# Two layers of message passing on a graph: 56 of the 98 tiles of the table relu(LN(x))·W0 made inside the loop of the first block, not ahead of it

## The chip, the cores and the metric

One Trainium2 chip, one core. The number is the device time of one execution in microseconds (us), as a median over runs. The engines are TensorE (PE, with its weight loads as PEld), VectorE (DVE), ScalarE (ACT), GpSimd (POOL) and SyncE (SP). Each works through its own list of instructions in order and waits for others by semaphores. POOL issues the gathers and scatters (indirect DMAs), SP issues the plain DMAs.

## The reference

There are N = 12500 nodes of D = 256 numbers and E = 200000 edges (`src`, `dst`, sorted by `dst`). The distribution of `dst` is dense at small numbers: it is 12500·u² of a uniform u.

```python
h = relu(layernorm(x))
x = x + segment_sum(edge_weight[:, None] * (h @ W0)[dst], src, N)      # layer 0
h = relu(layernorm(x))
q, k, v = h @ Wq.T + bq, h @ Wk.T + bk, h @ Wv.T + bv                  # 8 heads of 32
sim = (q[dst] * k[src]).sum(-1) / sqrt(32)                             # layer 1
attn = softmax of sim over the edges with the same dst
x = x + segment_sum(attn * v[src], dst, N) @ Wo.T + bo
```

## The kernel before

The edges are cut into 391 groups of 512, and the groups into four blocks of 128 (the last block has 7). The order of the instructions on PE, DVE, ACT, POOL and SP is written out by hand, that is, it is the order of the Python calls in `layer0` and `layer1`. What one call issues stands on each engine behind what the calls ahead of it issued there.

**The stretch ahead of the gathers** (`layer0`, the loop `while rest or live`). Three things run interleaved. `sort(0)` sorts block 0 by `src`: some 130 stages, each of them three compares on DVE (L237, L240, L241), a copy of the values on ACT (`vp`, L235) and a predicated copy on DVE (L247). At the larger distances the tile is transposed: 8 transposes on PE, and copies out of PSUM on ACT (L280, L282) or DVE (L265). `hidden()` makes the table HW = relu(x − mean)·W0 / sd, 98 tiles of 128 nodes, in 25 chunks of four tiles, at 85 steps of 100. Per tile it takes the sum and the squares on ACT (L569, L580; for one tile in four `bn_stats` on DVE, L572), subtracts the mean on POOL (`norm`, L596), transposes on PE (`turn`, L602), copies with relu on ACT (`turned`, L607), multiplies on PE (`mult`, L613) and copies with the factor 1/sd on ACT (`put`, L619). Per chunk there is one load and one store on SP. `group_l0` does the 7 groups of the last block, which are not sorted, with scatters on POOL. The first gather needs `dT` (L291), which the sort leaves.

**The loop of layer 0** (`for t in range(NGS + 6)`) has 120 + 128 + 128 steps. In block 0 a step has three tiles of 128 sorted edges, in blocks 1 and 2 four. Step t issues the gathers of step t + 4 on POOL (`load_s`, L648; six buffers `hg`), makes the one-hot matrices of step t + 1 on DVE (`onehot_s`, L657, which read `iop`, a row of numbers in a PSUM bank), multiplies gathered rows and one-hots on PE (`sum_s`, L668, and L667 for the last row of the window ahead), copies the window to `wn` for that (ACT, L689) and adds it to rows of an accumulator (`store_s`, DVE L694), which SP loads (`window_s`) and stores. Beside this runs the sort of the next block, 1.2 stages a step in block 0 and 1.14 in block 1, from step 4 of the block on. From t = 66 to 236 there are also 152 "hot" tiles, edges with `dst` below 128, whose rows come from a matrix product with the first 128 rows of HW (`hot_load`, `hot_ones`, `hot_pair`, `hot_apply`, `hot_add`, `hot_store`); those 128 rows are loaded over `w0[:, 0]` ahead of the loop. `prep_s` prepares layer 1 at t = 154, 174, 194 and 214. In block 2 `project_s` makes K and V of each finished window and stores them (`put`, L737, through two buffers `K`).

**Layer 1** has 391 steps and 1564 gathers of K and V (L978, 15 buffers `kvt`). Its last part merges the rows at the ends of the groups (`merge_steps`). There `same`, at step NG − 2, makes matrices that say which group ends are the same node (L1199 to L1210) and a mask (L1213 to L1216). These live in buffers of the tile `kvt`.

Of the kernel before, what the change touches and what calls it, by code (L numbers as in the profile page):

```python
# [18 lines left out]
P = 128  # L19
G = 512  # L20
# [37 lines left out]
H0, H1 = 66, 236  # L58
# [23 lines left out]
class Gnn:  # L82
# [30 lines left out]
    def sort_consts(self, it, ic):  # L113
        nc, kp = self.nc, self.k0
        ev = kp.tile([P, 1], I32, name="ev")
        nc.vector.tensor_scalar(ev, ic, 1, None, op0=ALU.bitwise_and)
        self.sgn = kp.tile([P, 1], F32, name="sgn")
        nc.vector.tensor_scalar(self.sgn, ev, -2.0, 1.0, op0=ALU.mult, op1=ALU.add)
        gr = kp.tile([P, P], I32, name="gr")
        nc.vector.tensor_scalar(gr, it, 1, None, op0=ALU.logical_shift_right)  # L120
        nc.vector.tensor_tensor(gr, gr, it, op=ALU.bitwise_xor)
        self.turn = kp.tile([P, 7, P], F32, name="turn")
        for j in range(7):
            bt = kp.tile([P, P], I32, name="bt", bufs=2)
            nc.vector.tensor_scalar(bt, gr, j, 1, op0=ALU.logical_shift_right, op1=ALU.bitwise_and)
            nc.vector.tensor_scalar(self.turn[:, j], bt, -2.0, 1.0, op0=ALU.mult, op1=ALU.add)
        self.iop = self.tp.tile([P, G], F32, name="iop")[:, :P]
        nc.vector.tensor_copy(self.iop, self.iof)
# [44 lines left out]
    def prep_c(self, b):  # L173
# [22 lines left out]
        ci = self.csi[b] = cp.tile([P, P, W], I32, name=f"ci{b}")  # L196
# [13 lines left out]
    def sort(self, b):  # L210
# [86 lines left out]
        if b == 0:  # L297
            nc.scalar.copy(self.in_order(eT), self.by_col(V))
            yield
# [61 lines left out]
    def tile_bases(self, dT, sf, eT, turned):  # L361
# [11 lines left out]
        self.fm = k0.tile([P, 9], F32, name="fm0")  # L373
        nc.vector.memset(bs[:, NHT:NHT + 1], float(BIAS))
# [16 lines left out]
    def hot_prep(self):  # L391
        nc, k0, wp = self.nc, self.k0, self.wp
        dT, eT, sT, _, _ = self.part[0]
        bs, fm, n = self.hb, self.fm, NHT
        nc.vector.memset(bs[:, 0:1], float(HBIAS))
# [18 lines left out]
        nc.vector.tensor_reduce(self.fl[:, 0, 0:1], fm[:, :8], op=ALU.max, axis=AX.X)  # L414
# [28 lines left out]
    def hot_apply(self, j):  # L443
        self.nc.tensor.matmul(self.hp[j][:, D:], self.ha.pop(j)[:, 0], self.w0[:, 0], start=True, stop=True)
# [89 lines left out]
    def hidden(self):  # L534
# [4 lines left out]
        chunks = list(range(nch - 2, nch)) + list(range(nch - 2))  # L539
        seq = [i for c in chunks for i in range(c * HC, min(nt, (c + 1) * HC))]  # L540

# [51 lines left out]
        def norm(i):  # L593
            c, j, r = tile_of(i)
            h = T[i]["h"] = wp.tile([P, D], F32, name="h", bufs=3)
            nc.gpsimd.tensor_scalar(h[:r], X[c][:r, j], M[c][:r, j, 0:1], None, op0=ALU.add)  # L596

        def turn(i):
            r = tile_of(i)[2]
            pt = T[i]["pt"] = tp.tile([P, G], F32, name="pt", bufs=1)[:, :D].rearrange("p (k e) -> p k e", e=P)  # L600
# [8 lines left out]
        def mult(i):  # L609
            r = tile_of(i)[2]  # L610
            ph = T[i]["ph"] = self.bank()[:, :D]
# [3 lines left out]
        def put(i):  # L615
# [4 lines left out]
            if j == HC - 1 or i == nt - 1:  # L620
                v, n = rows(self.HW, c)
                nc.sync.dma_start(v, Y[c][:, :n])
                if r < P:
# [8 lines left out]
        for s in range(nt + 8):  # L632
            for f, k in fs:
                if 0 <= s - k < nt:
                    f(seq[s - k])
            yield

# [5 lines left out]
    def load_s(self, g):  # L643
# [3 lines left out]
        for w, (c, _) in enumerate(self.tiles(b, p)):  # L647
            nc.gpsimd.indirect_dma_start(out=hg[:, w], out_offset=None, in_=self.HW,  # L648
                                         in_offset=bass.IndirectOffsetOnAxis(ap=self.part[b][0][:, c:c + 1], axis=0))
# [41 lines left out]
    def store_s(self, g):  # L691
# [5 lines left out]
        if b == NPT - 1:  # L697
            self.X[g] = dict(x=ws, base=v)
# [5 lines left out]
    def project_s(self, t):  # L704
# [30 lines left out]
        def put(X):  # L735
            kv = wp.tile([P, G], F32, name="K")
# [170 lines left out]
    def prep_s(self, b):  # L907
# [27 lines left out]
        self.nsl[b] = self.kp.tile([P, P, W], F32, name=f"nsl{b}")  # L935
# [7 lines left out]
        nc.sync.dma_start(self.PD[b * 2 * P:(b + 1) * 2 * P].rearrange("(p c) -> p c", c=2), gb[:, 1:3])  # L943
        nc.vector.tensor_tensor(t, pf, df, op=ALU.is_gt)
# [216 lines left out]
    def merge_steps(self):  # L1161
# [19 lines left out]
        def loads():  # L1181
            b = big(2 * KB * P)
            pdr, S = b[:, :KB * P], b[:, KB * P:].rearrange("p (k e) -> p k e", k=KB)
# [7 lines left out]

        def same():
            pdr, S, pdc = T["pdr"], T["S"], T["pdc"]
            cnt = wp.tile([P, KB], F32, name="cntm", bufs=1)
            tr = wp.tile([P, KB], F32, name="trm", bufs=1)
            scr = wp.tile([P, P], F32, name="scrm", bufs=1)
            T["idx"] = wp.tile([P, KB], I32, name="idxm", bufs=1)
            T["nid"] = wp.tile([P, KB], I32, name="nidm", bufs=1)
            nc.vector.tensor_scalar(T["nid"], pdc, 0.0, None, op0=ALU.max)  # L1199
            T["C"] = big(KB * P, KB)  # L1200
            for k in range(KB):
                r, m = size(k), pdr[:, rows(k)]
                if k:
                    nc.vector.tensor_scalar(T["C"][:, k], m, pdc[:, k - 1:k], self.ident[:, size(k - 1) - 1:size(k - 1)],
                                            op0=ALU.is_equal, op1=ALU.mult)
                nc.vector.tensor_scalar(S[:, k, :r], m, pdc[:, k:k + 1], None, op0=ALU.is_equal)
                nc.vector.scalar_tensor_tensor(scr[:, :r], S[:, k, :r], 1.0, self.lower[:, :r], op0=ALU.mult, op1=ALU.mult,
                                               accum_out=cnt[:, k:k + 1])
            nc.vector.tensor_scalar(tr, cnt, 0.0, self.trash, op0=ALU.is_gt, op1=ALU.mult)
            nc.vector.tensor_tensor(T["idx"], tr, pdc, op=ALU.max)  # L1210
            b = big(2 * NR + 2)
            mk, f = b[:H, :NR + 1], b[:H, NR + 2:]
            nc.vector.memset(mk[:, 0:1], NEG)  # L1213
            nc.vector.memset(mk[:, NR:], NEG)
            nc.vector.tensor_tensor(mk[:, 1:NR], pdr[:H, 1:NR], pdr[:H, :NR - 1], op=ALU.not_equal)
            nc.vector.tensor_scalar(mk[:, 1:NR], mk[:, 1:NR], NEG, None, op0=ALU.mult)  # L1216
# [39 lines left out]
        def total(k):  # L1256
# [8 lines left out]
            if k:  # L1265
                q = size(k - 1)
                nc.tensor.matmul(pg[:r], T["C"][:q, k, :r], T["ms"][:q, k - 1], start=False, stop=True)
# [18 lines left out]
        def ends_put(k):  # L1286
# [6 lines left out]
        steps = [((NG - 3, 0), loads), ((NG - 2, 0), same), ((NG - 1, 0), load_rows), ((NG, 1), own_rows),  # L1293
                 ((NG + 1, 0), lambda: space("ms", D + H)), ((NG + 2, 0), lambda: space("o", D)),
                 ((NG + 4, 0), factors), ((NG + 4, 2), factor_cols), ((NG + 4, 2), lambda: space("an", D)),
                 ((NG + 5, 0), lambda: space("at", D)), ((t + 1, 0), load_rest)]
        for k in range(KB):
# [177 lines left out]
    def layer0(self):  # L1475
        tc, nc = self.tc, self.nc
        ET = mybir.EngineType
        with tc.tile_pool(name="k0", bufs=1) as self.k0, tc.tile_pool(name="w0", bufs=2) as self.wp, \
# [28 lines left out]
            with tc.manual_schedule(engines={ET.SP, ET.PE, ET.DVE, ET.Activation, ET.Pool}):  # L1507
# [6 lines left out]
                rest = [self.KS, self.hidden()]  # L1514
                s, gs, live = 0, [], None
                while rest or live:
                    for f in list(rest):
                        if (f is self.KS or s * 85 % 100 < 85) and next(f, self) is self:
                            rest.remove(f)
# [20 lines left out]
                nc.sync.dma_start(self.w0[:, 0], self.HW[:P])  # L1540
# [3 lines left out]
                job, quota, hq, hl = None, 0.0, [], 0  # L1544
                for t in range(NGS + 6):
                    b, p = sblk(t) if t < NGS else (NPT, t - NGS)
                    due = min(NHT, max(0, round((t - H0) * NHT / (H1 - H0))))
                    if hq:
# [12 lines left out]
                    if job is not None and p > 3:  # L1561
                        quota += 1.2 if b == 0 else 1.14
                        while quota >= 1.0:
                            quota -= 1.0
                            if next(job, self) is self:
                                job, quota = None, 0.0
                                break
                    if t + 2 < NGS and (sblk(t + 2)[0] < 2 or b == 2 and p > 0):
# [23 lines left out]
                    if todo_hot:  # L1592
                        self.hot_apply(hj)
                        if hj + 1 < NHT:
                            self.hot_ones(hj + 1)
                    self.project_s(t)
                    for f in todo.get(t, []):
                        f()
                    if t >= 122 and t % 2 == 0 and fill2:
                        fill2.pop(0)()  # L1600
                assert self.hs == NHT and not hq
                assert job is None and not fill and not fill2

    def run(self, hook=lambda k, n: None):
# [3 lines left out]
        with ExitStack() as es:  # L1608
# [7 lines left out]
            self.HW = self.dp.tile([N, D], F32, name="HW")  # L1616
            self.SL = self.dp.tile([NG, G], U8, name="SL")
# [5 lines left out]
            self.AG = self.dp.tile([N + P, D + H], F32, name="AG")  # L1623
            self.fl = cp.tile([P, NBLK, 2], F32, name="fl")
# [52 lines left out]
```

## Time and profile before

| | us |
|---|---|
| median of 12 runs (4285.13 to 4302.65) | 4292.26 |
| the profiled execution | 4303.72 |
| its span, first to last instruction | 4301.7 |
| first gather of layer 0 (start) | 357.2 |
| last gather of layer 0 (start) | 2122.9 |
| first and last gather of layer 1 (start) | 2150.4 and 4190.0 |

| engine | busy us | share |
|---|---|---|
| PE | 3459.6 | 80% |
| DVE | 3406.4 | 79% |
| POOL | 2985.0 | 69% |
| ACT | 2205.4 | 51% |

The profile is of one execution. Busy time is the union of an engine's instructions; a wait is the idle time ahead of an instruction, put down to what ended last. A 32-bit matmul shows as two passes, so the 1384 products of gathered tiles show as 2768.

### The profile page before, as it was taken

The numbers are of one execution on the slowest core, as the hardware profiler recorded it, in microseconds if no ns is written. First come the engines' busy times: TensorE is split into PE (matmuls) and PEld (weight loads), VectorE is DVE, ScalarE is ACT, GpSimd is POOL, SyncE is SP. The second block draws the span as 40 slices with busy tenths as digits, with TensorE's granted clock in tenths as the row PEclk, the third lists the DMA queues.
The fourth block names the chain that finished last, engine by engine and source line by source line (L and its number), as shares of the span: only waits on it lengthen the run. The fifth ranks groups of instructions, "written<-read, shape, count | busy, mean of one in ns | idle before, by whom it ended". The sixth has DMA issues, their size and how long they took to land. (4 is left out here: it accounts for less than half of the span.)

```text
span 4301.7 us, 61889 instructions
## 1 busy us (share of the span) xinstructions
PE 3459.6 (80%) x14078; PEld 2309.5 (54%) x14078; DVE 3406.4 (79%) x7226; ACT 2205.4 (51%) x6200; POOL 2985.0 (69%) x3096
## 2 busy tenths in 40 slices
PE   3665678786777789999868888888888888888886
PEld 2443335454444444444456666666666666666664
DVE  7878989697898666666558878788888888888895
ACT  5664345343443222222236666666666666666663
POOL 2555777677776777777567777777777777777771
PEclk9888999898998899999969999999999999999998
DMA  6434667786776788888688989889988888888892
GB/s 203 105 99 140 179 187 228 210 241 193 218 222 199 217 237 250 251 239 236 207 242 270 281 269 277 276 276 282 281 270 282 275 280 271 273 263 266 278 291 77
DMA packets 627547, 1004.38 MB, mean 233 GB/s; under 512 B 97274, under 2 KB 450359, under 8 KB 627165
## 3 DMA queue, kind: packets, MB, share of 16 engines
q0 software_dynamic: 196224, 596.49, 47.9%
q1 hardware_dynamic: 430941, 403.79, 29.3%
q8 instruction: 119, 1.95, 0.2%
q14 instruction: 263, 2.15, 0.2%
HBM read 788.60 MB, written 224.47 MB: 236 GB/s over the span
## 5 line engine op out<-in xcount | busy, mean ns | idle before, releaser
L978 POOL DMA_INDIRECT kvt<-KV,ci x1564 | 1501.5, 960 | 565.7 <-issue 405.9
L648 POOL DMA_INDIRECT hg<-HW,dT x1384 | 1314.9, 950 | 469.2 <-issue 355.2
L668 PE MATMUL pg<-hg,ohs 128*128 128x256 f32 x2768 | 875.7, 424 | 191.7 <-DMA hg<-HW,dT 80.4
L1089 PE MATMUL pg<-pv,oh 128*82 128x264 f32 x3126 | 845.3, 418 | 19.8 <-DVE pv L1077 16.6
L668 PEld LDWEIGHTS pg<-hg,ohs 128*128 128x128 f32 x2768 | 474.8, 197 | 585.3 <-DMA hg<-HW,dT 220.4
L1011 PE MATMUL pq<-qt,oht 80*128 80x256 f32 x3128 | 771.5, 391 | 8.1 <-ACT oht L987 8.1
L1011 PEld LDWEIGHTS pq<-qt,oht 80*128 80x128 f32 x3128 | 615.4, 198 | 117.7 <-ACT oht L987 9.3
L1089 PEld LDWEIGHTS pg<-pv,oh 128*82 128x82 f32 x3126 | 507.1, 165 | 257.0 <-issue 65.3
L1012 DVE TENSOR_TENSOR pr<-pq,kvt 128x512 f32<-128x512 f32 x782 | 514.4, 684 | 160.7 <-PE pq L1011 153.4
L995 ACT ACTIVATE oh<-iof,nsl 128x82 f32<-128x82 f32 x1564 | 437.3, 350 | 261.4 <-PE pg L1089 259.6
L657 DVE TENSOR_SCALAR ohs<-iop,sT,eT 128x128 f32<-128x128 f32 x1384 | 475.3, 410 | 39.8 <-PE pg L668 39.8
L1077 DVE TENSOR_TENSOR pv<-kvt,pp 128x1024 f32<-128x1024 f32 x391 | 471.4, 1206 | 34.4 <-ACT pb L1066 34.4
L1013 DVE TENSOR_REDUCE sim<-pr 128x32 f32<-128x1024 f32 x391 | 477.1, 1220 | 13.4
L986 ACT ACTIVATE oht<-slt,npcol 80x512 f32<-80x512 uint8 x391 | 281.9, 721 | 103.6 <-PE pq L1011 56.1
L689 ACT COPY wn<-pg 128x256 f32<-128x256 f32 x373 | 138.4, 371 | 279.7 <-PE pg L668 279.6
L471 ACT ACTIVATE sd<-mv,eps 128x1 f32<-128x1 f32 x128 | 37.7, 295 | 470.3 <-DVE sd L476 459.6
L827 PE MATMUL pq<-wtq,qh 128*128 128x256 f32 x392 | 133.7, 473 | 159.1 <-DMA qh<-HT 131.6
L987 ACT ACTIVATE oht<-oht 80x512 f32<-80x512 f32 x391 | 246.3, 630 | 12.7
L247 DVE COPY_PREDICATED W<-m,vp 128x512 f32<-128x512 int32 x317 | 232.6, 734 | 18.7 <-ACT vp L235 18.5
L715 PE MATMUL tps<-wkv,ht 128*128 128x512 f32 x512 | 240.7, 593 | 0.0
L737 DVE TENSOR_TENSOR K<-tps,bias 128x512 f32<-128x512 f32 x128 | 88.6, 692 | 185.0 <-PE tps L715 182.2
L235 ACT COPY vp<-W 128x512 f32<-128x512 f32 x344 | 203.2, 591 | 61.7 <-DVE W L247 50.9
(304 smaller groups left out, 4558.3 us busy)
## 6 DMA issues: line engine op xcount, KB each, us to landing
KV<-K SPq DMA_DIRECT2D x128, 256.0 KB
AG<-ag SPq DMA_DIRECT2D x391, 82.5 KB
tw<-acc SPq DMA_DIRECT2D x248, 128.0 KB
acc<-ws SPq DMA_DIRECT2D x248, 128.0 KB
qt<-Q SPq DMA_DIRECT2D x391, 80.0 KB
kvt<-KV,ci POOLq DMA_INDIRECT x1564
hg<-HW,dT POOLq DMA_INDIRECT x1384
xh<-acc SPq DMA_DIRECT2D x152, 128.0 KB
```

The lines of the kernel that those rows point to most:

```text
L648: nc.gpsimd.indirect_dma_start(out=hg[:, w], out_offset=None, in_=self.HW, in_offset=bass.IndirectOffsetOnAxis(ap=self.part[b][0][:, c:c + ...
L657: self.nc.vector.tensor_scalar(oh[:, w], self.iop, sT[:, c], eT[:, c], op0=ALU.is_equal, op1=ALU.mult)
L668: nc.tensor.matmul(pg, oh[:, w], hg[:, w], start=(w == 0), stop=(w == n - 1))
L978: nc.gpsimd.indirect_dma_start(out=kv[:, w], out_offset=None, in_=self.KV, in_offset=bass.IndirectOffsetOnAxis(ap=self.csi[b][:, p, w:w + ...
L986: nc.scalar.activation(oht, sl, AF.Abs, bias=self.npcol[:QW])
L987: nc.scalar.activation(oht, oht, AF.Relu, bias=1.0, scale=-1.0)
L995: nc.scalar.activation(oh[:, w], self.iof[:, :MA], AF.Abs, bias=self.nsl[b][:, p, w:w + 1])
L1011: nc.tensor.matmul(pq[:, c], oht[:, 2 * a + c], qt, start=True, stop=True)
L1012: nc.vector.tensor_mul(pr[:, 2 * a:2 * a + 2], pq, kv[:, 2 * a:2 * a + 2, :D])
L1013: nc.vector.tensor_reduce(sim[:, :, i, :], pr.rearrange("p w (h d) -> p w h d", h=H), op=ALU.add, axis=AX.X)
L1077: self.nc.vector.tensor_tensor(pv[:, :, :D].rearrange("p w (h d) -> p w h d", h=H), kv[:, :, D:].rearrange("p w (h d) -> p w h d", h=H), s ...
L1089: nc.tensor.matmul(pg, oh[:r, w], pv[:r, w], start=(w == 0), stop=(w == nw - 1))
```

## The change

The table is made in two parts. Ahead of the loop `hidden` now makes 42 tiles only: the last two chunks (6 tiles), which `group_l0` needs, and the first nine (36 tiles). It runs in every step of the sort up to 24 and then in 40 of 100. The first three chunks (1536 rows) are also stored to a table of their own, HA. Block 0 gathers from HA, by `dA`, which is `dT` cut off at 1535; a flag (`far`) sends inputs with larger `dst` there to the general path. The other 56 tiles are made in the loop of layer 0, from t = 5 to 80, by `table(pos, t)` at three places of a step: `mult` at the start, the statistics, `norm` and `put` after the sort's stages, `turn` and `turned` at the end. In these tiles `norm` is on ACT, and the transposed tile and the product lie in the free columns of the PSUM bank of `iop`, one after the other. The hot tiles start at t = 84 rather than 66; their 128 rows have a tile of their own. K and V are stored through four buffers (`K` and `W`) rather than two. In layer 1 `same` is cut into seven parts, at steps 296 + 9k, which write over parts of `nsl` and `ci` that are no longer read; the mask is made in `prep_s` and loaded.

```diff
-H0, H1 = 66, 236
+H0, H1 = 84, 236
+NHA = 12
+HT0, HT1 = 5, 81
+NHS = 6
...
-        self.iop = self.tp.tile([P, G], F32, name="iop")[:, :P]
+        self.iopt = self.tp.tile([P, G], F32, name="iop")
+        self.iop = self.iopt[:, :P]
...
             nc.scalar.copy(self.in_order(eT), self.by_col(V))
+            self.dA = self.l0r.bitcast(I32)
+            nc.vector.tensor_scalar(self.dA, dT, float(NHA * P - 1), None, op0=ALU.min)
...
+        far = wp.tile([P, G], F32, name="pf", bufs=1)
+        nc.vector.tensor_tensor(far, dT, self.dA, op=ALU.not_equal)
+        nc.vector.tensor_reduce(fm[:, 8:9], far, op=ALU.max, axis=AX.X)
...
-        chunks = list(range(nch - 2, nch)) + list(range(nch - 2))
+        na = NHA // HC
+        first = list(range(nch - 2, nch)) + list(range(na + NHS))
+        chunks = first + list(range(na + NHS, nch - 2))
         seq = [i for c in chunks for i in range(c * HC, min(nt, (c + 1) * HC))]
+        ns = sum(min(nt, (c + 1) * HC) - c * HC for c in first)
+        late = set(seq[ns:])
...
-            nc.gpsimd.tensor_scalar(h[:r], X[c][:r, j], M[c][:r, j, 0:1], None, op0=ALU.add)
+            if i in late:
+                nc.scalar.activation(h[:r], X[c][:r, j], AF.Identity, bias=M[c][:r, j, 0:1])
+            else:
+                nc.gpsimd.tensor_scalar(h[:r], X[c][:r, j], M[c][:r, j, 0:1], None, op0=ALU.add)
...
-            pt = T[i]["pt"] = tp.tile([P, G], F32, name="pt", bufs=1)[:, :D].rearrange("p (k e) -> p k e", e=P)
+            T[i]["pp"] = self.iopt[:, P:P + D] if i in late else tp.tile([P, G], F32, name="pt", bufs=1)[:, :D]
+            pt = T[i]["pt"] = T[i]["pp"].rearrange("p (k e) -> p k e", e=P)
...
-            ph = T[i]["ph"] = self.bank()[:, :D]
+            ph = T[i]["ph"] = T[i]["pp"] if i in late else self.bank()[:, :D]
...
                 nc.sync.dma_start(v, Y[c][:, :n])
+                if c < na:
+                    nc.sync.dma_start(rows(self.HA, c)[0], Y[c][:, :n])
...
+        ls = ((mult, 7, 0), (root, 3, 1), (scale, 4, 1), (stats, 0, 1), (square, 2, 1), (norm, 5, 1), (put, 7, 1),
+              (turn, 6, 2), (turned, 6, 2))
+        n = nt - ns
+        for s in range(n + 7):
+            for pos in range(3):
+                for f, k, at in ls:
+                    if at == pos and 0 <= s - k < n:
+                        f(seq[ns + s - k])
+                yield
...
-            kv = wp.tile([P, G], F32, name="K")
+            kv = wp.tile([P, G], F32, name="KW"[X["g"] % 2])
...
+        me = wp.tile([P, 2], F32, name="me")
+        nc.vector.tensor_tensor(me[:, 0:1], pf[:, 0:1], base, op=ALU.not_equal)
+        nc.vector.tensor_copy(me[:, 1:2], ne)
+        nc.vector.tensor_scalar(me, me, NEG, None, op0=ALU.mult)
+        nc.sync.dma_start(self.ME[b * 2 * P:(b + 1) * 2 * P].rearrange("(p c) -> p c", c=2), me)
...
+        def same(k):
+            S, pdc, cnt = T["S"], T["pdc"], T["cnt"]
+            r, m = size(k), T["pdr"][:, rows(k)]
+            scr = wp.tile([P, P], F32, name="scrm", bufs=1)
+            nc.vector.tensor_scalar(S[:, k, :r], m, pdc[:, k:k + 1], None, op0=ALU.is_equal)
+            nc.vector.scalar_tensor_tensor(scr[:, :r], S[:, k, :r], 1.0, self.lower[:, :r], op0=ALU.mult, op1=ALU.mult,
+                                           accum_out=cnt[:, k:k + 1])
+            if k:
+                q = size(k - 1)
+                nc.vector.tensor_scalar(m, m, pdc[:, k - 1:k], self.ident[:, q - 1:q], op0=ALU.is_equal, op1=ALU.mult)
...
-        steps = [((NG - 3, 0), loads), ((NG - 2, 0), same), ((NG - 1, 0), load_rows), ((NG, 1), own_rows),
+        steps = [((286, 1), loads), ((366, 0), own_ids), ((NG - 2, 0), load_mask), ((NG - 1, 0), load_rows), ((NG, 1), own_rows),
...
+        steps += [((296 + 9 * k, 0), lambda k=k: same(k)) for k in range(KB)]
...
-                    for f in list(rest):
-                        if (f is self.KS or s * 85 % 100 < 85) and next(f, self) is self:
-                            rest.remove(f)
+                    if going:
+                        going = next(self.KS, self) is not self
+                    if not self.ready and (s < 24 or s * 40 % 100 < 40 or not going):
+                        next(HT)
...
+                def table(pos, t):
+                    nonlocal late, made
+                    goal = (3 * (NQ - NHA - 2 - HC - HC * NHS) + 21) * (t - HT0 + 1) / (HT1 - HT0)
+                    while late and made < goal and (pos is None or made % 3 == pos):
+                        made += 1
+                        late = next(HT, self) is not self
+                        if pos is not None:
+                            break
```

## The prediction

> **What bounds the kernel now.** I read the waits of POOL first, then POOL's timeline, then the windows by stage, then DVE's waits ahead of the first gather, and last DVE's timeline at the end.
>
> The timeline of POOL in block 0 (start, duration, engine, line, operation, idle before):
>
> ```profile
> 562.68 0.95 POOL L648 DMA_INDIRECT hg<-HW,dT  x1 [0.30 <-issue]
> 563.93 0.95 POOL L648 DMA_INDIRECT hg<-HW,dT  x1 [0.30 <-issue]
> 565.18 0.95 POOL L648 DMA_INDIRECT hg<-HW,dT  x1 [0.30 <-issue]
> ```
>
> Gathers start every 1.25 us. POOL shows 76% busy (0.95 of 1.25) when it cannot go faster, so its 69% hides the bound. The waits of POOL over the whole span (in total, times, longest):
>
> ```profile
> POOL kvt L978 <- issue: 405.9, 1332, 0.3
> POOL hg L648 <- issue: 355.2, 1166, 0.3
> POOL kvt L978 <- DVE pv L1077: 84.0, 75, 7.9
> POOL hg L648 <- PE pg L668: 50.2, 65, 7.0
> ...
> POOL hg L648 <- DVE dT L291: 17.5, 1, 17.5
> ```
>
> The 0.3 us waits for "issue" are part of the rhythm. 1384 gathers at 1.2545 us are 1736 us, and from the first (357.2) to the last (2122.9) it is 1766: POOL lost some 30 us in all of layer 0. Layer 1 is alike: 1564 at 1.2545 are 1962 of 2040 us. So three things set the time: when the first gather starts, how often a late consumer blocks POOL, and the end after the last gather at 4190. The windows by stage (length; busy us and instructions of PE, PEld, DVE, ACT, POOL; clock; DMA share and GB/s):
>
> ```profile
> 8.90:357.20 348.30, 196.26 (x820) 145.43 (x820) 277.06 (x774) 229.59 (x679) 153.83 (x126) 0.85 0.46 125
> 357.20:836.30 479.10, 356.93 (x1383) 204.61 (x1383) 422.31 (x1193) 199.96 (x528) 357.56 (x378) 0.92 0.67 197
> 836.30:1495.60 659.30, 485.92 (x2048) 304.75 (x2047) 534.22 (x1502) 248.85 (x701) 481.72 (x506) 0.88 0.74 214
> ```
>
> Ahead of the gathers DVE is the bound (277 of 348 us). In block 0 POOL's 357.6 us at 76% are 470 of 479 us; DVE is at 88%, so there is little room beside it.
>
> **The change, part by part.**
>
> *The stretch ahead of the first gather: −34 us.* DVE's waits there:
>
> ```profile
> DVE m L237 <- ACT K L280: 19.0, 5, 6.3
> DVE W L247 <- ACT vp L235: 18.5, 26, 3.1
> DVE K L265 <- PE tps L252: 14.7, 7, 5.6
> ```
>
> 14 of 25 chunks leave. Their four DVE instructions (0.40, 0.18, 0.19, 0.16 us) start one behind the other in some 0.76 us a chunk: −11. The waits for `vp` mostly go with the load on ACT: −7. The twelve waits at the sort's transposes (33.7 us) hold a part that is the sort's own: the short ones among them are 0.9 to 1.4 us. Twelve at 1.1 and 4 us for what stays beside them leave 17: −17. `dA` (0.4) and the full rate up to step 24 add 1. Sum −34. Bounds: −20 if the transposes keep their waits but for a few us, −46 if half of DVE's 70 us of gaps there goes as well as the 11 us. POOL's `norm` (121 us busy here) costs nothing either way, since POOL has no gather to issue yet.
>
> *The 56 tiles in block 0: +41 us.* POOL's pace is 3 × 1.254 = 3.76 us a step. The consumer's own pace is DVE's: three one-hots at 0.32, a stage of the sort at 1.60 (starts at 563.99, 564.31, 564.64, 564.97, 565.59) and the window's add 0.33, so 2.9 us with one stage and 4.5 with two, as the steps of the trace show. What a late tile adds, by the same work ahead of the gathers (lines view, 0 to 500 us):
>
> ```profile
> L613 PE MATMUL pg<-w,ht 128*128 128x256 f32 (+1 forms) x392 | 125.6, 452 | 1.4 <-ACT yh L619 1.4
> L619 ACT ACTIVATE yh<-pg,sd 128x256 f32<-128x256 f32 x98 | 46.2, 472 | 9.5 <-PE pg L613 9.4
> L607 ACT ACTIVATE ht<-pt 128x256 f32<-128x256 f32 x98 | 37.2, 380 | 2.2 <-PE pt L602 2.2
> L602 PE MATMUL pt<-ident,h 128*128 128x128 f32 x196 | 48.2, 335 | 119.8 <-ACT ht L607 73.5 <-POOL h L596 30.5 <-issue 15.7
> ```
>
> The product takes 1.28 us, the two transposes 0.49, the relu copy 0.38, the scaled copy 0.47; both PE parts use one region of PSUM. In the built order a full step is a ring: PE's `mult` waits for `turned` of the step before; then stands `sum_s`; then `turn`, which waits for `put`; then `turned` on ACT. `put` stands on ACT behind the sort's copies and the statistics, and it waits for DVE's one-hots, which wait for `mult` (all touch the bank of `iop`). With one stage: 1.28 + sum_s 2.2 (three products at 0.55, the carry 0.59) + 0.49 + 0.38 = 4.35. The lower end is 3.85, with passes at 0.216 us as the quickest in the trace; I take 4.25. With two stages ACT decides: after `turned`, mult 1.3, one-hots 1.0, compares 1.1, predicated copy 0.7, `vp` of the second stage 0.6, statistics and `norm` 1.0 (0.31 to 0.51 apiece), `put` 0.47, `turn` 0.5, `turned` 0.4: 7.0 us.
>
> The loop's rate (189 calls in 76 steps, each place in turn) gives, after seven steps that only fill the pipe, 45 full steps, 10 of them with two stages, and 12 pairs of steps that share one round (6.3 us the pair, against 7.52). So 35 × (4.25 − 3.76) = 17, 10 × (7.0 − 3.76) = 32, pairs −15 (POOL is behind, so what they win is used), nine transposing stages of the sort of block 1, some in pairs, 7 × 1.9 = 13 (8 transposes and the later copies), and −6 for slack in the gather buffers and the quick first steps: +41. Bounds: +10 (3.85; 5.9 with two stages, the ring without the one-hots' 1.1; half the transposes) to +80 (4.9 us in every full step, if passes run at 0.29 us, the median here, and transposes in full). This stall is POOL's: it holds gathers, and all later ones shift by it.
>
> The one-hots wait for PE's products of gathered tiles alone today (39.8 us in all). The Trainium skill, "PSUM — Partial Sum Buffer", section "PSUM bank collisions raise a hardware error", says that two engines may not be on one bank at once even at other columns, so accesses must be kept apart by semaphores. That speaks against putting the tiles beside `iop`: by the rule a step with two stages costs 7.0, without it the first stage need not wait for `mult` and it is about 5.9, 11 us less in all. No row of this trace shows two engines on one bank.
>
> *Queues it is moved past.* SP gets 14 loads and 14 stores more among the windows' transfers, 0.6 us each to issue, 17 us in 286; DMA gets 14.7 MB, 51 GB/s on 197, where layer 1 carries 274. 0, up to +8 if a window load behind them is late. The hot tiles from 84 spare 18 steps some 0.6 us and are denser later; POOL was blocked 7 us by them up to t = 108, and would be again: 0 (−3 to +5).
>
> *Rest of layer 0: +6.* The four `prep_s` get some 0.4 us of DVE, and the 116 steps of block 1 carry 1.0 hot tiles and not 0.89 (DVE 0.65 each), so after each `prep_s` (steps of 19 to 33 us) some 1.4 us less is caught up: 0 to +10. More buffers for K and V: `put` waited 182 us for PE and nothing else that shows: 0 (−3 to 0).
>
> *Layer 1: +4, end −7.* The cover of the seven parts is DVE's slack (1664 of 2040 us busy), but POOL waits for `pv` 75 times, so part of 7 × 0.9 us shows: 0 to +6. The end (DVE's timeline):
>
> ```profile
> 4198.63 0.17 DVE L1199 TENSOR_SCALAR nidm<-pdc 128x7 int32<-128x7 f32 x1
> ...
> 4205.29 0.56 DVE L1216 TENSOR_SCALAR kvt<-kvt 8x781 f32<-8x781 f32 x1
> 4205.77 0.40 DVE L877 TENSOR_TENSOR o<-pq,ox 128x256 f32<-128x256 f32 x1
> ```
>
> From 4198.6 to 4205.8 DVE does nothing else, and the next similarity waits behind it: −7 (−4 to −9).
>
> Sum: −34 + 41 + 0 + 6 + 4 − 7 = +10. The profiled execution took 4303.7 (span 4301.7 and 2.0 around it) and would take 4313.7; it lies 11.4 above the median, so the median goes from 4292.3 to 4302.
>
> **Rivals.** *The ring is covered* (faster): steps with one stage at 3.85 cost 3, those with two at 5.9 cost 21, transposes 9, pairs −15, slack −6, so block 0 loses 12 and the sum is −19: 4273. For it: six gather buffers, and steps as short as 1.6 us late in block 0. Against it: the ring has one PSUM region. It decides from a loss in block 0 below some 22 us. *PE's slower passes* (slower): block 0 loses 75, +44: 4336. For it: passes of 0.43 us in the trace where the clock is lower; against it: a clock of 0.92 in this block. *The sort keeps its waits*, so that the shorter stretch isn't what the change makes of it: −20, sum +24: 4316. For it: the longest waits are at the transposes; against it: those are 4 to 6 us only where ACT and PE also carry `hidden`.
>
> **How the numbers follow.** Forecast 0.45, ring covered 0.33, slower passes 0.12, sort's waits 0.10. A change within 0.2% (8.6 us) can't be told from none. Faster: 0.33 and 0.03 of the forecast's low end; within: 0.20 of the forecast; slower: 0.22 + 0.12 + 0.10. The forecast's own range is 4283 to 4322; with the rivals 4262 to 4345.
>
> **What would show it.** First gather at 323 us (above 337: the first step is wrong). Steps from t = 12 to 80 of 4 to 4.5 us, with 7 at two stages, and POOL waits for PE's `pg` of some 40 us there. Last gather of layer 0 at 2136, and 7 us less after the last gather of layer 1. I am wrong if POOL keeps 1.25 us through block 0.

## The result, and the profile after

| | before | after |
|---|---|---|
| median, us | 4292.26 (46 runs) | 4357.63 (11 runs, 4336.8 to 4371.94) |
| ratio, after to before | | 1.0151, 95% interval 1.0136 to 1.0166 |
| the profiled execution | 4303.72 | 4342.15 |

The changed kernel is 1.5% slower. The forecast was 4302 us with a range up to 4345; slower was its likeliest sign, but the loss is larger than the range held.

The profiled execution of the changed kernel is one of its quickest. Two more profiles of it (e16 and e17 below) took 4362.2 and 4379.9 us, and e16 lies near the median. So the table of where the time goes has both beside the execution before. A "late" tile is one of the 56 that are made in the loop. "Stall" is the sum, over the gathers, of the time by which the distance to the gather ahead exceeds 1.2545 us, the pace of the prediction; a step is three gathers in block 0 and four in the others.

| us | before | after | e16 | predicted difference |
|---|---|---|---|---|
| first gather | 357.2 | 322.4 | 329.2 | −34 |
| stall, steps up to 80 | 0.5 | 74.0 | 73.5 | +41 |
| stall, steps 81 to 120 | 6.8 | 17.6 | 17.7 | 0 |
| stall, block 1 | 27.6 | 23.2 | 32.3 | +6 |
| last gather of layer 0 to first of layer 1 | 27.5 | 29.6 | 30.0 | 0 |
| layer 1, first to last gather | 2039.6 | 2038.2 | 2040.9 | +4 |
| from the last gather to the end | 111.6 | 103.1 | 105.4 | −7 |
| span | 4301.7 | 4340.2 | 4360.2 | +10 |

In the lines of the changed kernel, a late tile is L620 (`turn`), L625 (`turned`), L631 (`mult`) and L637 (`put`); the gathered tiles are L681 (gather), L690 (one-hots), L701 (product) and L727 (the window's add).

The first gathers of the changed kernel (timeline of POOL: start, duration, engine, line, operation, idle before with what ended it):

```profile
322.43 1.01 POOL L681 DMA_INDIRECT hg<-HA,l0r  x1 [59.41 <-DVE l0r L304]
323.74 0.97 POOL L681 DMA_INDIRECT hg<-HA,l0r  x1 [0.30 <-issue]
```

They start at 322.4 us instead of 357.2, and wait for the sort on DVE (L304) now as before. The step that was meant to be shorter is shorter. What it gives is lost again further on; the waits of POOL over the whole span show where (in total, times, longest):

```profile
POOL hg L681 <- issue: 353.1, 1159, 0.3
POOL hg L681 <- PE pg L701: 89.6, 74, 6.4
POOL kvt L1016 <- DVE pv L1115: 82.9, 68, 4.5
...
POOL hg L681 <- PE iop L620: 49.3, 19, 7.4
```

The wait of layer 1 for `pv` (84.0 us before) is as it was. The wait of gathers for PE's `pg` rises from 50.2 to 89.6 us, and a new one of 49.3 us stands beside it: POOL waits for `turn` (L620), which is the transpose of a late tile. It doesn't use that tile. It waits for a gather buffer, and the products that free the buffer are followed in PE's order by `turn`, which the view names because it ended last. The two together are 88.7 us more than before, near the 74 − 0.5 + 17.6 − 6.8 = 84 of the table.

Inside the stretch of the late tiles, first the window (length; busy us and instructions of PE, PEld, DVE, ACT, POOL; granted clock; DMA share and GB/s), then the largest waits of DVE and PE's weight loads:

```profile
384.00:728.00 344.00, 261.27 (x954) 150.85 (x951) 238.97 (x664) 194.04 (x559) 199.85 (x212) 0.89 0.58 171
```

```profile
DVE ohs L690 <- PE iop L631: 83.9, 46, 4.0
...
PEld iop L620 <- ACT yh L637: 48.9, 36, 3.7
```

No engine is full: PE is at 76%, DVE at 69%, ACT at 56%, and POOL's 199.85 us at 76% busy are 263 of 344 us of gathers. DVE, PE and ACT wait for one another in turn. The largest of these waits is that of DVE's one-hots for the product `mult` of a late tile (L631), 46 times 1.8 us. The one-hots don't use this product. They read `iop`, which lies in the same PSUM bank, and the program's semaphores make them wait until the product is done.

The end shows the other gain (timeline of DVE, after the last gather at 4237.1):

```profile
4241.92 1.21 DVE L1115 TENSOR_TENSOR pv<-kvt,pp 128x1024 f32<-128x1024 f32 x1
4243.06 0.42 DVE L910 TENSOR_TENSOR o<-pq,ox 128x256 f32<-128x256 f32 x1
...
4244.17 1.28 DVE L1050 TENSOR_TENSOR pr<-pq,kvt 128x512 f32<-128x512 f32 x2
```

Where the matrices of `same` held DVE for 7 us between two similarities, there is some 1 us now.

### The profile page after: what moved, and what is told of

It reads as the page before. It is cut to its first block, busy times and chain, and to the rows that moved or that the text cites. A ratio compares the mean times of both kernels' runs of the same rounds, so it can differ in the third digit from the quotient of the medians.

```text
span 4340.2 us, 61901 instructions
## 1 busy us (share of the span) xinstructions
PE 3473.7 (80%) x14078; PEld 2317.1 (53%) x14078; DVE 3402.5 (78%) x7239; ACT 2229.2 (51%) x6256; POOL 2921.6 (67%) x3040
## 5 line engine op out<-in xcount | busy, mean ns | idle before, releaser
L681 POOL DMA_INDIRECT hg<-HW,dT x1024 | 975.2, 952 | 331.3 <-issue 267.2
L701 PE MATMUL pg<-hg,ohs 128*128 128x256 f32 x2768 | 872.0, 423 | 125.0 <-DMA hg<-HW,dT 43.5
L701 PEld LDWEIGHTS pg<-hg,ohs 128*128 128x128 f32 x2768 | 479.1, 198 | 501.1 <-issue 207.2
L690 DVE TENSOR_SCALAR ohs<-iop,sT,eT 128x128 f32<-128x128 f32 x1384 | 475.1, 408 | 119.5 <-PE iop L631 83.9
L681 POOL DMA_INDIRECT hg<-HA,l0r x360 | 340.8, 947 | 260.1 <-issue 85.9
L700 PE MATMUL pg<-wn,cs 128*1 128x256 f32 x746 | 229.7, 390 | 1.0 <-ACT wn L722 1.0
```

Source lines behind the costliest of these rows:

```text
L690: self.nc.vector.tensor_scalar(oh[:, w], self.iop, sT[:, c], eT[:, c], op0=ALU.is_equal, op1=ALU.mult)
L701: nc.tensor.matmul(pg, oh[:, w], hg[:, w], start=(w == 0), stop=(w == n - 1))
```

## The experiments

The theory after the result: the late tiles are the whole loss, and it is made by the order that the shared bank sets (one-hots behind `mult`, `put` behind the one-hots), so that steps become a ring of DVE, PE and ACT, in which each waits for the one before. Rivals: the loss is PE's (its work, its passes); it is the wait of `put` for the reciprocal alone; or it is something else of the change (queues, hot tiles, the tables, layer 1).

A round is the time from one late tile's `turn` to the next one's. It is a full step (all of a late tile's work in one step of the loop) or a pair of steps that share this work, and it holds one or more stages of the sort. "First", "stall to 80" and "81 to 120" are as in the table above, of the profiled execution, which need not lie near the median: that of e2 is its slowest (4377.4 us, its layer 1 some 33 us longer than before), that of e12 its quickest (4295.9). The ratios are to runs of the kernel before on the same chip (median 4302.4 us for e1 to e4, 4306.0 for e9 to e12, 4306.8 for e16 to e18).

| run | first | stall to 80 | 81 to 120 | median us | ratio, 95% interval |
|---|---|---|---|---|---|
| e1_all_ahead | 357.6 | 0.5 | 0.0 | 4306.7 | 1.0004 [0.9982, 1.0027] |
| e2_scale_first | 329.3 | 60.0 | 15.6 | 4354.4 | 1.0103 [1.0073, 1.0132] |
| e3_own_bank | 328.8 | 18.4 | 13.1 | 4315.7 | 1.0024 [1.0003, 1.0045] |
| e4_74_ahead | 344.2 | 12.1 | 11.3 | 4320.0 | 1.0039 [1.0020, 1.0057] |
| e9_onehots_from_sbuf | 327.6 | 17.2 | 4.8 | 4298.6 | 0.9987 [0.9972, 1.0003] |
| e10_own_bank_scale_first | 328.9 | 19.9 | 10.8 | 4309.7 | 1.0022 [1.0004, 1.0040] |
| e11_58_ahead | 337.8 | 0.4 | 8.9 | 4296.7 | 0.9971 [0.9950, 0.9993] |
| e12_early_put | 326.8 | 21.4 | 11.6 | 4322.9 | 1.0040 [1.0017, 1.0062] |
| e16_changed_third | 329.2 | 73.5 | 17.7 | 4363.2 | 1.0164 [1.0122, 1.0206] |
| e17_changed_fourth | 329.7 | 75.2 | 17.6 | 4379.9 (one run) | |
| e18_sbuf_58_ahead_2 | 335.6 | 0.9 | 1.2 | 4287.2 | 0.9963 [0.9944, 0.9981] |

**All tiles ahead** (e1). The late part of the table is empty; everything else of the change stays.

```diff
-NHS = 6
+NHS = 20
-... s * 40 % 100 < 40 ...
+... s * 85 % 100 < 85 ...
```

> All 98 tiles ahead of the gathers again, at 85 steps of 100 after step 24; every other part of the change stays (hot tiles from 84, HA, four buffers for K and V, end matrices in layer 1). If the late tiles are the whole loss: first gather at 356 to 360 us, POOL's stall in steps 5 to 81 under 3 us, the end some 8 us shorter, so 4283 to 4295 us, 0.998 to 1.001 of before. If another part of the change costs too (the moved matrices, the denser hot tiles): 4305 or more.

The time is that of the kernel before (1.0004), and the stall in block 0 is gone. So the late tiles are the whole loss, and what is left of the change (gathers from HA, the hot tiles' new place, four staging buffers, the matrices of `same`) is worth nothing that can be told from the interval: its end is 5.7 us shorter (105.9 against 111.6), its block 1 stalls 31.0 us instead of 27.6.

**The reciprocal ahead of the one-hots** (e2). `put` needs 1/sd of the chunk. In the changed kernel DVE makes it behind the sort's stages of the same step.

```diff
-ls = ((mult, 7, 0), (root, 3, 1), (scale, 4, 1), (stats, ...
+ls = ((mult, 7, 0), (scale, 4, 0), (root, 3, 1), (stats, ...
```

> One edit to the changed kernel: the reciprocal (scale) of a chunk of late tiles goes to the first place of the step, ahead of the one-hots, where it stood behind the sort on DVE and the scaled copy of the chunk's first tile waited for it. Theory of the round types: rounds with a chunk's first tile fall from 5.5 to 3.9 us (full) and from 9.6 to some 7.5 (pairs), 14 rounds, POOL's stall falls by 20 to 25 us from 74, 4330 to 4340 us. Rival, the shared PSUM bank alone: those rounds are no longer than others once the one-hots are counted, stall within 5 us of 74, 4350 to 4365 us.

14 us of the stall go, less than the 20 to 25 that the theory expected and more than the 5 of its rival. Most of it goes where this wait is: the nine rounds of a full step with one stage and the first tile of a chunk fall from 5.5 to 4.1 us. The pairs fall little (from 9.0 to 8.6 in the mean; with a chunk's first tile from 9.6 to 8.8, where 7.5 was expected).

**A bank of their own for the late tiles** (e3), the one that the tiles ahead of the loop use and, from t = 84, the hot tiles.

```diff
-T[i]["pp"] = self.iopt[:, P:P + D] if i in late else tp.tile([P, G], F32, name="pt", bufs=1)[:, :D]
+T[i]["pp"] = tp.tile([P, G], F32, name="pt", bufs=1)[:, :D]
```

> One edit to the changed kernel: the late tiles use the PSUM bank that the hot tiles use from t = 84 on, which is free until then, so the one-hots and the late tiles no longer share a bank. Rival, the shared bank is the loss: POOL's stall falls from 74 to under 15 us, 4285 to 4300 us. Theory of the round types: the region is still one, the floor of 3.9 us and the pairs stay; steps with two stages fall from 7.2 to some 6, the waits for the reciprocal from 5.5 to some 4.5, the stall falls to 45 to 55 us, 4325 to 4342 us.

The stall falls from 74 to 18.4 us, with the same instructions in the same order. This is close to the rival (under 15) and far from what I held (45 to 55): the shared bank makes most of the loss, and the price that I had set on it was too small.

**74 tiles ahead** (e4), the bank as in the change.

```diff
-NHS = 6
+NHS = 14
-... s * 40 % 100 < 40 ...
+... s * 60 % 100 < 60 ...
```

> 74 tiles ahead (60 steps of 100 after step 24) and 24 late, at the same steps 5 to 80, so that a late tile is spread over some 2.5 steps. If the loss goes with the number of full rounds: hardly a step has all three places, stall under 15 us, first gather 6 to 12 us later than with 42 ahead (330 to 336 us), 4283 to 4300 us. If every late tile has its price whatever its spread (1.3 us each): stall some 32 us, 4310 to 4325 us.

24 late tiles stall POOL 12.1 us, 0.5 us a tile where 56 cost 1.3. The first gather came at 344.2, later than expected. The time is above what these two would give. In the profiled execution, gathers started every 1.258 us rather than every 1.251; over its 2948 gathers that is 20 us. Whether the other eight runs had this pace too isn't shown.

**Four combinations, where PE was granted less** (e5 to e8). Own bank with the reciprocal first; one-hots from SBUF; 58 tiles ahead with both edits of e5; `table(1, t)` ahead of the sort's stages with both edits of e5.

> Both edits at once: the late tiles in the hot tiles' PSUM bank, and the reciprocal at the first place of the step. If the waits for the reciprocal still stand with the bank apart (rounds of a chunk's first tile 4.4 us against 4.2): the stall in steps 5 to 81 falls from 18 to 12 us, 0.9995 to 1.0025 of before. If the bank was all of it: the same as with the bank alone, 18 us, 1.0024.

> One edit to the changed kernel: the one-hots of the gathered tiles read the row of numbers from SBUF, not from the PSUM bank; the late tiles stay where they are, in the bank of that row. It takes the dependence away and moves no tile. If the dependence of the one-hots is the loss: stall in steps 5 to 81 of 15 to 25 us, rounds as with the bank apart, 1.001 to 1.005. If it was the place of the tiles (another buffer, its waits): 60 us or more, 1.012 or more. A third way: POOL's gathers come slower than every 1.25 us beside DVE's reads of SBUF, then the whole of layer 0 is longer (0.01 us a gather is 14 us).

> Bank apart, reciprocal first, and 58 tiles ahead (50 steps of 100 after step 24) with 40 late ones. First gather 4 to 10 us later than with 42 ahead, stall up to step 120 of some 12 us where it was 31 with the bank alone; 0.996 to 1.0005 of before if both add up, 1.002 if the stretch ahead takes it back.

> Bank apart, reciprocal first, and the second place of the step (statistics, norm, scaled copy) ahead of the sort's stages, where it stood behind them. If ACT's queue sets the rounds with two stages (5.4 us): they fall to some 4.8 and the stall from some 15 to under 10 us, 0.997 to 1.001. If DVE's stage, which then gets its copies 1.5 us later, sets them: no gain or a loss, stall over 20 us, 1.002 to 1.006.

Here the kernel before took 5425.1 us. The four took 5429.1, 5417.9, 5431.6 and 5430.8, and every interval holds 1.000. The granted clock was 0.82 to 0.83, and gathers stalled in every part of the program (some 750 us in layer 1 against 85), so that PE set the time and no stretch of block 0 could be seen in it. By themselves they say nothing on the question, and they were run again in another set, as e9 to e12.

**One-hots that read SBUF** (e9). The late tiles stay in the bank of `iop`. The one-hots of gathered tiles read the same row of numbers from its copy in SBUF, so that they touch this bank no more.

```diff
-self.nc.vector.tensor_scalar(oh[:, w], self.iop, sT[:, c], eT[:, c], ...
+self.nc.vector.tensor_scalar(oh[:, w], self.iof, sT[:, c], eT[:, c], ...
```

> The changed kernel with the one-hots of the gathered tiles read from SBUF, once more, since the chip of the first try granted PE so little that every kernel took 5400 us. On a chip like the first: stall in steps 5 to 81 of 15 to 25 us and 1.001 to 1.005 if the dependence of the one-hots on the bank is the loss; 60 us or more and 1.012 or more if it is the place of the tiles.

This moves no tile and no instruction, and takes one dependence away. The stall falls to 17.2 us, as with a bank apart, and the time, 0.9987 of before, is a little below what was expected. The same window as above, in this kernel:

```profile
384.00:728.00 344.00, 286.67 (x1183) 171.27 (x1182) 287.52 (x836) 228.38 (x661) 247.41 (x261) 0.98 0.72 213
```

In the same 344 us there are 261 gathers instead of 212, and PE does 24% more instructions in 10% more busy time. (The last 66 us of the window lie behind the last `turn` of this kernel, at 662 us; in the changed kernel it is at 718.) The waits of DVE and POOL in it:

```profile
DVE ohs L690 <- PE pg L701: 22.5, 28, 2.2
```

```profile
POOL hg L681 <- PE pg L701: 20.2, 27, 3.5
POOL hg L681 <- PE iop L620: 8.5, 10, 3.9
```

The 83.9 us of one-hots behind `mult` are gone, and POOL's two waits shrink from 49.3 and 45.8 to 28.7 us together. The timeline shows the order change hands (a step of this kernel):

```profile
546.14 0.85 DVE L690 TENSOR_SCALAR ohs<-iof,sT,eT 128x128 f32<-128x128 f32 x3
546.32 1.13 PE L631 MATMUL iop<-w,ht 128*128 128x256 f32 x4 [0.47 <-ACT ht L625]
```

The one-hots start 0.2 us before `mult` instead of some 0.1 us behind its end.

**Bank apart and reciprocal first** (e10; both edits shown above).

> Bank apart and reciprocal first, once more for the same reason: stall in steps 5 to 81 of 12 us and 0.9995 to 1.0025 if the reciprocal still costs with the bank apart, 18 us and 1.0024 if not.

19.9 us of stall against 18.4 for the bank alone. With the bank apart, the earlier reciprocal gains nothing in the stall, so its 14 us in e2 were a part of the same ring, and not a second cause.

**58 tiles ahead** (e11; the edits of e10, `NHS = 10` and 50 in place of 40).

> 58 tiles ahead, bank apart, reciprocal first, once more for the same reason: 0.996 to 1.0005 of before if the smaller stall and the later start add up to a gain, 1.002 if the stretch ahead takes it back.

40 late tiles in the same 76 steps leave no stall (0.4 us), and the first gather comes 9 us later than in e10. This version is 0.3% faster than the kernel before: 0.9971, with an interval that ends below 1.

**An earlier `put`** (e12; the edits of e10, and in the loop).

```diff
+                    table(1, t)
                     if job is not None and p > 3:
...
-                    table(1, t)
```

> Second place of the step ahead of the sort's stages, bank apart, reciprocal first, once more for the same reason: stall under 10 us and 0.997 to 1.001 if ACT's queue sets the rounds with two stages, over 20 us and 1.002 to 1.006 if DVE's stage does.

Rounds with two stages fall from 5.5 to 4.4 us, but the pairs of steps rise from 6.9 to 8.2: the sort's copies now stand behind the tile's work on ACT. The stall is what it was (21.4 against 19.9); why the median is 13 us above that of e10 isn't shown.

**The changed kernel again** (e13, e14, then e16, e17), for where its usual execution differs from the profiled one, and **SBUF one-hots with 58 tiles ahead** (e15, then e18): the edit of e9, `NHS = 10` and 50 in place of 40, nothing else. The first three met the conditions of e5 to e8 (5423.7 us for the kernel before).

> The changed kernel, nothing edited. If the profiled execution was a lucky one ahead of the gathers and in layer 1: first gather 327 to 329 us, stall of the gathers in the steps up to t = 80 again 70 to 80 us, layer 1 from first to last gather 2045 to 2065 us, execution 4350 to 4365, ratio 1.010 to 1.016. Rival, the ring itself varies: stall up to t = 80 of 85 to 105 us, layer 1 at 2038 to 2042.

> The changed kernel once more, for a third profile: as for e13, first gather 327 to 329 us, stall up to t = 80 of 70 to 80 us by the one theory, 85 to 105 us by the rival.

> One-hots of gathered tiles read their row of numbers from SBUF, and 58 tiles are made ahead (40 late), the tiles and the order of their operations as in the changed kernel. If the bank and the number of late tiles are the whole cause: first gather 337 to 339 us, stall up to t = 80 under 5 us, last gather of layer 0 at 2105 to 2112, ratio 0.995 to 0.999. Rival, the order of the reciprocal and the bank of the tiles matter too: stall up to t = 80 of 8 to 15 us, ratio 0.999 to 1.002.

Under these the changed kernel took 5464.1 us, 1.0067 [1.0043, 1.0092], with a stall of 127 and 125 us up to t = 80; e15 took 5422.6, 0.9997 [0.9975, 1.0020], with 86. Beside these, e5, e6 and e8 say something after all: they have the same 56 late tiles without the shared bank, and stall 84 to 89 us. So there too the bank costs some 40 us of stall, and 0.7% of the time; fewer late tiles (e7 with 79, e15 with 86) save little there.

> The changed kernel, nothing edited, on another chip (expectation as for e13). Lucky profile: first gather 327 to 329 us, stall up to t = 80 of 70 to 80 us, layer 1 2045 to 2065 us, ratio 1.010 to 1.016. Rival, the ring itself varies: stall up to t = 80 of 85 to 105 us, layer 1 at 2038 to 2042.

> The changed kernel once more: first gather 327 to 329 us, stall up to t = 80 of 70 to 80 us by the one theory, 85 to 105 us by the rival.

Both have 73.5 and 75.2 us of stall up to t = 80: the ring doesn't vary, and most of its rounds agree to 0.1 us between executions. What varies is the first gather (329.2 and 329.7; in five kernels above that are the same ahead of it, 326.8 to 329.3), block 1 (32.3 and 32.9 against 23.2) and, in e17 alone, layer 1 (2048.6) and the end (111.9). So 7 us ahead of the gathers and 9 us in block 1 of the first profile were luck, as the one theory had it, though layer 1 in e16 stayed at 2040.9, below what it expected.

> As e15, on another chip: if the bank and the number of late tiles are the whole cause, first gather 337 to 339 us, stall up to t = 80 under 5 us, last gather of layer 0 at 2105 to 2112, ratio 0.995 to 0.999. Rival, the order of the reciprocal and the bank of the tiles matter too: stall up to t = 80 of 8 to 15 us, ratio 0.999 to 1.002.

0.9 us of stall, the first gather at 335.6, the last of layer 0 at 2095.6 (2122.9 before, and 2105 to 2112 expected), and 0.9963: some 16 us below the kernel before, the lowest ratio of all, though its interval overlaps that of e11. Neither the order of the reciprocal nor another bank for the tiles is needed for it. The dependence on the bank and the number of late tiles are the whole cause of the stall up to t = 80.

## Why the prediction was right and wrong

**Right in the sum, not in its parts: the stretch ahead of the first gather.** −34 was −34.8 in the profile and −28 in e16 and e17, within its bounds (−20 to −46). DVE's waits from 0 to the first gather, first one of the kernel before that the prediction didn't show (to 357.2), then those of the changed kernel (to 322.4):

```profile
DVE W L244 <- ACT vp L235: 9.8, 2, 8.0
```

```profile
DVE W L251 <- ACT vp L239: 25.4, 16, 8.3
DVE m L241 <- ACT K L284: 10.1, 6, 3.0
DVE K L269 <- PE tps L256: 7.0, 7, 2.2
DVE W L248 <- ACT vp L239: 4.1, 3, 1.8
```

The waits at the transposes fell from 33.7 to 17.1 us, the −17 that were booked. Those for `vp`, booked at −7, did not fall: 28.3 us before, 29.5 after (33.2 in e16). DVE's busy time made up for it: it fell by 18 us (277.1 to 259.2), where 11 less 1 were booked. That these two errors cancel, and that the profile is quicker here than the others, is luck.

**Right: the end** (−7; −8.5 in the profile, −6.2 in e16, −3 to −7 in e1 to e4, e9 to e12 and e18; but +0.3 in e17). **Not decided: block 1** (+6; −4 in the profile, +5 in e16 and e17): executions of one kernel differ there by more than the term. **Right: the place.** POOL's waits were to be at PE, between t = 12 and 80, and they are, in part under the name of `turn`. The ring through one PSUM region that was to make them is in e9 too, and makes 17 us there.

**Wrong: the size of block 0**, +41 (bounds up to +80). The rounds of the ring, from one `turn` to the next, mean us:

| round | count | predicted | changed kernel | e16 | e9 |
|---|---|---|---|---|---|
| full step, one stage | 25 | 4.25, transposes apart | 4.56 | 4.58 | 4.29 |
| the same, first tile of a chunk | 9 | 4.25 | 5.53 | 5.52 | 4.32 |
| full step, two stages | 10 | 7.0 | 7.2 | 7.3 | 5.4 |
| pair of steps | 11 | 6.3 | 9.0 | 8.8 | 6.7 |

The step that failed is the one that says "12 pairs of steps that share one round (6.3 us the pair, against 7.52)" and books them at −15. There are 11, they take 9.0 us, and 11 × (8.99 − 7.52) = +16: an error of 31 of the 33 us. (Two of them, of 11.1 and 9.3 us, hold transposes that the prediction booked apart; the other nine take 8.7.) Full steps with one stage, with the sort's transposes in them, cost 25 × 0.80 + 9 × 1.77 = 36 us against 17 + 13 = 30, those with two stages 10 × 3.42 = 34 against 32, and the slack took 12 us off instead of 6; the sum is 74. With the one-hots off the bank (e9), pairs take 6.7 us, and 9 of the 15 us come.

Why pairs are long is seen in the timeline of the changed kernel. First a pair without transposes, then the step in which the first tile of a chunk is put:

```profile
494.99 0.38 PE L620 MATMUL iop<-ident,h 128*128 128x128 f32 x2
...
495.85 1.13 PE L631 MATMUL iop<-w,ht 128*128 128x256 f32 x4 [0.47 <-ACT ht L625]
...
497.09 1.05 DVE L690 TENSOR_SCALAR ohs<-iop,sT,eT 128x128 f32<-128x128 f32 x3 [1.38 <-ACT sd L600]
...
499.66 0.41 DVE L727 TENSOR_TENSOR ws<-pg,tw 128x256 f32<-128x256 f32 x1
...
500.17 1.10 PE L701 MATMUL pg<-hg,ohs 128*128 128x256 f32 x4 [1.18 <-issue]
...
502.26 0.38 PE L620 MATMUL iop<-ident,h 128*128 128x128 f32 x2
...
557.08 0.17 DVE L605 RECIPROCAL sd<-sd 128x4 f32<-128x4 f32 x1
...
557.33 0.47 ACT L637 ACTIVATE yh<-iop,sd 128x256 f32<-128x256 f32 x1 [2.13 <-PE pg L701]
```

`mult` ends at 496.98, and the one-hots start 0.1 us behind it, after 1.38 us in which DVE idles (the view puts this wait down to the last event, `sd`, but it ends with `mult`). Then DVE does its stage of the sort, and only then the window's add (L727, 499.66). PE's products for the next step (500.17) begin 0.1 us behind this add, which frees their bank (the view names nothing for this wait, but `L694` for the like wait in the kernel before), 1.18 us after PE was free. I had counted the pair as two steps of PE and DVE work around one round of the ring. I had not followed what DVE does behind the one-hots: the wait that the bank sets delays the stage, the stage delays the add, and the add delays the second step's products, which stand ahead of the next `turn`. The shortest pairs take 7.3 us. At 557.08 the same delay meets a second order that I had left out: `put` of a chunk's first tile needs the reciprocal, which stands behind the stage on DVE. It ends at 557.25, and `put` starts at 557.33, 2.1 us after ACT was free (the view puts this wait down to a product that had ended 0.9 us before; e2 shows that it is the reciprocal's). That makes 5.5 us of a round of 3.9, and 9.6 of a pair.

**The price of the rule on the banks.** The prediction set 11 us on it: 1.1 us in ten steps with two stages. Against e9 it is 10 × 1.8 = 18 us there, 11 × 2.3 = 25 in the pairs, 9 × 1.2 = 11 at the chunks' first tiles and 25 × 0.27 = 7 in the other steps, 61 in all, of which 74.0 − 17.2 = 57 show in the stall. The Trainium skill, "PSUM — Partial Sum Buffer", section "PSUM bank collisions raise a hardware error", says that two engines must be kept apart on one bank, where they touch the same partitions, even at other columns. The trace shows a program that keeps to this: one-hots waited 83.9 us for products in columns that they don't read. No run here lets two engines on one bank at once, so what the chip itself would do isn't shown. The prediction had the order of the program right, at the wrong price.

**The rivals.** "PE's slower passes" named a loss of 75 us in block 0, which is the size, but not by its cause: 16 of the 25 full steps with one stage and no first tile of a chunk are at 3.8 to 3.9 us, the lower end of the prediction, and not at 4.9. The clock in this stretch was lower than before (0.89 against 0.95; first the kernel before in the middle of its block 0, then e1):

```profile
417.00:675.00 258.00, 188.51 (x693) 95.98 (x692) 234.77 (x639) 108.05 (x275) 195.14 (x207) 0.95 0.65 188
```

```profile
384.00:728.00 344.00, 253.38 (x910) 125.15 (x910) 312.61 (x854) 140.05 (x352) 260.18 (x276) 0.95 0.64 185
```

In e9 the clock is 0.98 with more work on PE, so the tiles themselves don't lower it; but with PE busy 73 to 74%, less than the 76% of the changed kernel, the two rows above have 0.95, so PE's idle share doesn't set it either. What set it is open. What part of the 57 us it had isn't separated, but an upper estimate comes from the passes: between the first and the last `turn`, those of products that follow one another at once came every 0.29 us on average in the changed kernel and every 0.26 in e9, so the 748 products' passes there cost at most some 22 us more. "The ring is covered" was wrong for this kernel and about right for the stall of e9 (17 us, where it had 12), not for its time (0.9987 of before, an interval that holds 1).

**Not foreseen: +11 us in steps 81 to 120.** The sum had 0 (up to +5 for hot tiles). They come in the same seven steps in all three profiles of the changed kernel. In steps 83 to 90 it is 8.6 us, where the kernel before has none; these are gone in e1, e11 and e18, where POOL was not held up before, and e3 and e9 keep 1 to 2 us of them. That the gather buffers' slack, used up by then, is what hides such steps fits this; no run shows it alone. In steps 101 to 117 it is 8.7 us against 6.7 before; these are gone in e1 and e18 but not in e11 (8.7), so for them the cause stays open.

By the terms of the prediction, e16 is then −28 + 73 + 11 + 5 + 4 (layer 1 and the way into it) − 6 = +59, which is its span's 58.5; for the first profile −35 + 74 + 11 − 4 + 1 − 8 = +39 against 38.5.

## What to carry to other kernels

Free columns of a PSUM bank aren't free if another engine uses the bank in every step: ask which instruction of which engine then stands between which others, and follow what is queued behind the one that waits, through every engine, until the ring closes. Work that is spread over a loop should be costed by its longest kind of step, and steps that share a round are the ones to follow instruction by instruction, since a gain booked there has no slack to come from. And a loop that is at its pace takes as much extra work as fits: here 40 tiles left no stall once the bank was out of the way, and 56 left 17 us. Other splits cost little to try; 40 need not be the best.

## What the runs showed of the hardware that was not expected

- The passes of PE's products that follow one another at once come mostly at 0.216, 0.32 or 0.43 us. Between 384 and 728 us it was 59, 22 and 12% of them in the changed kernel, with PE busy 76% of the time and a granted clock of 0.89; in e9 67, 25 and 3%, with PE busy 83% and 0.98. PE's busy share doesn't explain the clock: in e1 it was 74% there, at 0.95.
- The kernel before took 4292 to 4307 us (medians) in four sets of runs, and 5424 and 5425 in two others, where the granted clock was 0.82 to 0.83. In the profile of e5 the clock was at half for 1862 of 5417 us, in that of the kernel before for 728 of 4302.
- Three one-hots of 128x128 took 0.85 us from SBUF and 1.05 from PSUM, and POOL's gathers kept their pace of 1.251 us (median) beside them in e9 and e18; the mean of the distances under 1.4 us was 1.255, against 1.252 in the changed kernel.
- In one execution (e4) all gathers, in both layers, started every 1.258 us instead of 1.251: 20 us of the time from 0.5% of one engine's pace.
